# Four linked edits at the start and inside the last layer of a four-layer graph network: where input blocks are scaled, where two blocks' last sums stand, and which group's products come first

## The chip, the cores and the metric

The kernel runs on one core of a Trainium2 chip. The metric is the device time of one launch in microseconds; the time before is the median of three runs. Beside these runs there is one profiled execution, from which all views are taken. Five engines work side by side: TensorE (PE, matrix products; its weight loads are shown apart as PEld), VectorE (DVE), ScalarE (ACT), GpSimd (POOL) and SyncE (SP), which here only issues DMAs.

## The reference

The input x has 128 graphs of 64 nodes with 256 features. Four layers follow one another, each as `x = layernorm(x + layer(x))`: an attention layer, a multi-head edge attention, a graph convolution with two batch norms, and a last layer:

```python
h = relu(einsum('ts,bsh->bth', adj, x @ Wg0 + bg0))
h = relu(einsum('ts,bsh->bth', adj, h @ Wg1 + bg1))
for p in range(1, 5):                       # window length
    nw = T // p
    wins = h[:, :nw * p, :].reshape(B * nw, p, H)
    last = lstm_last(Wih[p-1], Whh[p-1], bih[p-1], bhh[p-1], wins)   # p steps, zero start
    h = h.at[:, arange(nw) * p + (p - 1), :].set(last)
```

The input of the last layer is the layer norm of the third layer's output, and that output ends in a batch norm, `out * scale + shift` for each feature. All of this is float32. The edits lie in the last layer alone.

## The kernel before

**Blocks, groups and pairs.** The nodes are worked on in 16 blocks of 512 rows (8 graphs each). Two blocks make a group of 16 graphs, two groups a pair; there are four pairs, and pair k takes blocks 4k to 4k+3. A tile `H` holds the hidden state of one pair, with the two groups side by side, and an LSTM step is computed for both groups.

**A block's way into the LSTM.** The generator `gcn` (L957) prepares one block in steps, each ending in a `yield`. Its first step issues the loads: two DMAs for the residual `x2r` (L964), and for blocks from 4 on one DMA for the third layer's output (L966). Blocks 0 to 3 have that output in SBUF already (tile `A0`, shown as A; `NA` is 4). Then for each half `a` of the block, `fetch` scales the output in place by the batch norm (two ACT instructions, L972, one for each 128 features) and turns it to have the nodes on partitions: blocks 0 to 3 by PE transposes (L979), later blocks by `turned`, which goes through DRAM. `norm` adds the residual (DVE, L985), makes the layer norm (DVE L95 to L98, POOL L86 and L100) and stores the result for later (two DMAs, L990). After both halves follow: sums over neighbours (PE L953 in `neighbours`, copied out at L1010 by DVE and L1011 by ACT), the first product in two steps (PE L1017, DVE L1019, ACT L1021), the second in two steps (PE L1029, DVE L1032), and the **last sums** over neighbours (PE L953 again), which DVE (L1040) and ACT (L1041) write into `H`. So a block of 0 to 3 has nine steps: load, two halves, sums, two, two, last sums. Blocks 0 and 2 (of these four) use PSUM banks named g, of which there are two; blocks 1 and 3 use banks named l, of which there are six, shared with the LSTM.

**The LSTM.** `lstm(pair)` yields a unit number after each piece of work. Window length 1 has units 0 to 7: units 0 to 3 serve group 0, units 4 to 7 group 1, each twelve matmul records of L1066. Lengths 2, 3 and 4 follow. The first step of such a run has no hidden state yet: `plain` (L1163) computes three gates from the input alone (PE L1174), for each half `m` of the output features and each group `g` a sum of two products, one for each half `k` of the input features. At lengths 2 and 4 both groups of one `m` share a bank (`joint`), at length 3 each has its own. Later steps (L1209) use a scheme with seven products per gate. `output` writes the state of the last step back into `H` (DVE L1139), for each half and group, in the order (m0,g0), (m1,g1), (m0,g1), (m1,g0); the next window length's `plain` reads `H`. A float32 matmul is two records in the trace.

**Order.** What an engine issues is set by a scheduler, except that `given` (L852) puts the instructions of each step behind the last one issued before on the same engine. It does so for PE, DVE, ACT and POOL, not for SP. The first blocks are advanced by a hand-written list of block numbers (L1367), one step for each entry; after the whole list come the loads of the first LSTM weights (wx and wh, L891). Blocks 2 and 3 finish as side work of pair 0, at units given by `put` (L1381). Steps put at one unit run in the order of the `put` calls.

Of the kernel before, what the change touches and what calls it, by code (L numbers as in the profile page):

```python
# [11 lines left out]
AF = mybir.ActivationFunctionType  # L12
# [9 lines left out]
KD = D // P  # L22
# [6 lines left out]
QT = 512  # L29
# [12 lines left out]
def kernel(ctx: ExitStack, tc: tile.TileContext, i, out):  # L42
    nc = tc.nc
# [44 lines left out]
    def layernorm(dst, src, n, engine):  # L88

        st = small.tile([P, n, 6], F32, name="ln_st", bufs=5)  # L90
        mv = small.tile([P, n, 2], F32, name="ln_mv", bufs=5)
        both = small.tile([P, 2, n], F32, name="ln_rs", bufs=5)
        rs, ng = both[:, 0, :], both[:, 1, :]
        for r in range(n):
            nc.vector.bn_stats(st[:, r, :], src[:, r, :])  # L95
            nc.vector.bn_aggr(mv[:, r, :], st[:, r, :])
        rsqrt(rs, mv[:, :, 1], n)
        nc.vector.tensor_scalar_mul(ng, mv[:, :, 0], -1.0)  # L98
        for r in range(n):
            engine.tensor_scalar(dst[:, r, :], src[:, r, :], ng[:, r:r + 1], rs[:, r:r + 1],  # L100
                                 op0=OP.add, op1=OP.mult)
# [13 lines left out]
    with ExitStack() as two:  # L115
# [13 lines left out]
        def bank(shape, name="m", bufs=3):  # L129
            return (psm if name == "m" else ps).tile([P] + shape, F32, name=name, bufs=bufs)  # L130
# [571 lines left out]
        sc2, sh2 = (const.tile([P, M2], F32, name=n) for n in ("sc2", "sh2"))  # L702
# [11 lines left out]
        def hidden(q, m):  # L714
            return Z[q][:, m, :] if m < 2 else Aq(q)[:, (m - 2) * QT:(m - 1) * QT]
# [16 lines left out]
        def put(q, m, p_):  # L732
            nc.scalar.activation(hidden(q, m), p_, AF.Identity, bias=b1[:, m:m + 1])
# [29 lines left out]
        bias = wd.tile([P, SKIP, 8], F32, name="bias")  # L763
# [167 lines left out]
    def turned(src):  # L931


        t = work.tile([P, 4, 4, 32], F32, name="st", bufs=ST)
        nc.vector.transpose(t, src.rearrange("p n (j t) -> p j n t", t=32))
        o = work.tile([P, 4, 4, 32], F32, name="st", bufs=ST)
        way = dram.tile([P, 4, P], F32, name="way", bufs=4)
        nc.sync.dma_start(way, t.rearrange("p j n f -> p j (n f)"))
        for j in range(4):
            nc.sync.dma_start(o[j * 32:(j + 1) * 32].rearrange("t i n f -> t i (n f)"),  # L940
                              way[:, j, :].rearrange("(i t) x -> t i x", t=32))
        return o.rearrange("p i (c m) f -> p c m i f", m=KD)
# [14 lines left out]
    def gcn(g, half, bank, name):  # L957

        q = g * 2 + half
        here = A0[:, q % NA, :]  # L960
        x2r = []
        for a in range(2):
            x2r.append(work.tile([P, 2, D], F32, name="x2r", bufs=4))
            nc.sync.dma_start(x2r[a].rearrange("p c d -> p (c d)"), x2_dram[q][:, a * 2 * D:(a + 1) * 2 * D])  # L964
        if q >= NA:
            nc.sync.dma_start(here, z_dram[q])  # L966
        yield

        def fetch(a):
            z = here[:, a * QT:(a + 1) * QT].rearrange("p (c m t) -> p c m t", c=2, m=KD)  # L970
            for m in range(KD):
                nc.scalar.activation(z[:, :, m, :], z[:, :, m, :], AF.Identity,  # L972
                                     bias=sh2[:, m:m + 1], scale=sc2[:, m:m + 1])
            if q >= NA:
                return turned(z.rearrange("p c m t -> p (c m) t"))
            xt = bank([2, D])
            for m in range(KD):
                for c in range(2):
                    nc.tensor.transpose(xt[:, c, m * P:(m + 1) * P], z[:, c, m, :], ident)  # L979
            return xt  # L980

        def norm(a, xt):
            x = x2r[a]
            xv = x.rearrange("p c (m i f) -> p c m i f", m=KD, f=32) if q >= NA else x
            nc.vector.tensor_add(xv, xt, xv)  # L985
            x3 = here[:, a * QT:(a + 1) * QT].rearrange("p (c d) -> p c d", c=2)
            layernorm(x3, x, 2, nc.gpsimd)
            for c in range(2):
                b0 = q * GQ + a * 4 + c * 2
                nc.sync.dma_start(x3_dram[b0:b0 + 2].rearrange("s t d -> (s t) d"), x3[:, c, :])  # L990

        if q >= NA:
            came = []
            for a in range(2):
                came.append(fetch(a))
                yield
            for a in range(2):
                norm(a, came[a])
                yield
        else:  # L1000
            for a in range(2):
                norm(a, fetch(a))
                yield

        x3 = here.rearrange("p (c d) -> p c d", c=PQ)
        p_ = neighbours(bank, lambda c, f: x3[:, c, f:f + 64])
        own = work if name == "hT" else late
        hT = own.tile([P, KD, QT], F32, name=name, bufs=2)
        dst = hT.rearrange("p k (c s n) -> p s (k c) n", c=PQ, s=2)
        nc.vector.tensor_copy(dst[:, 0], p_[0].rearrange("p k c n -> p (k c) n"))  # L1010
        nc.scalar.activation(dst[:, 1], p_[1].rearrange("p k c n -> p (k c) n"), AF.Copy)  # L1011
        yield
        hN = own.tile([P, KD, QT], F32, name=name, bufs=2)
        for m in range(KD):
            p_ = bank([PQ, P])
            for k in range(KD):
                nc.tensor.matmul(p_.rearrange("p c t -> p (c t)"), wg[0][:, k, m * P:(m + 1) * P], hT[:, k, :],  # L1017
                                 start=k == 0, stop=k == KD - 1)
            nc.vector.tensor_add(hN[:, m, :].rearrange("p (c t) -> p c t", c=PQ), p_,  # L1019
                                 rb[:, m:m + 1, :].to_broadcast([P, PQ, P]))  # L1020
            nc.scalar.activation(hN[:, m, :], hN[:, m, :], AF.Relu)  # L1021
            yield
        ys = []
        for a in range(2):
            p_ = bank([2, D])
            for c in range(2):
                t = (2 * a + c) * P
                for k in range(KD):
                    nc.tensor.matmul(p_[:, c, :], hN[:, k, t:t + P], wg[1][:, k, :],  # L1029
                                     start=k == 0, stop=k == KD - 1)  # L1030
            y = work.tile([P, 2, D], F32, name="st", bufs=ST)
            nc.vector.tensor_add(y, p_, bg1[:, None, :].to_broadcast([P, 2, D]))  # L1032
            ys.append(y)
            yield
        p_ = neighbours(bank, lambda c, f: ys[c // 2][:, c % 2, f:f + 64])

        if g // 2 not in Hs:
            Hs[g // 2] = input_tile()
        dst = Hs[g // 2][:, g % 2].rearrange("p k t (h c s) -> p h s k c t", h=2, s=2)[:, half]
        nc.vector.tensor_scalar_max(dst[:, 0], p_[0], 0.0)  # L1040
        nc.scalar.activation(dst[:, 1], p_[1], AF.Relu)  # L1041
        yield
# [4 lines left out]
    def lstm(pair):  # L1047
# [36 lines left out]
        for p in range(2, SKIP + 1):  # L1084
# [78 lines left out]
            def plain(n, r, tiles):  # L1163

                t = tiles[n] = rows()
                at, _ = gate_of(n)
                for m in (1, 0):
                    f, b = bias_of(n, m)
                    joint = 2 * nw * GB <= QT
                    banks = lbank([2, nw, GB]) if joint else None  # L1170
                    for g in range(2):
                        one = banks[:, g] if joint else lbank([nw, GB])
                        for k in range(KD):
                            nc.tensor.matmul(one, w.raw[0][:, k, at, m, :], inp(r, 0, k)[:, g],  # L1174
                                             start=k == 0, stop=k == KD - 1)
                        if not joint:
                            nc.scalar.activation(t[m][:, g], one, f, bias=b)
                    if joint:
                        nc.scalar.activation(t[m], banks, f, bias=b)
                for m in (1, 0):  # L1180
                    finish(n, r, 0, tiles, m)
                    tanh(n, tiles, m)
# [180 lines left out]


    parts = [gcn(n // 2, n % 2, gbank if n % 2 == 0 else lbank, "hT" if n % 2 == 0 else "xs") for n in range(4)]
    first = [prepare(weights_of[0, p]) for p in (2, 3)]
    for n in [0, 1, 0, 0, 1, 1, 0, 1, 0, 1, 2, 0, 1, 2, 0, 1, 3, 2, 0, 1, 0, 1, 3, 2, 3]:  # L1367
        given(next, parts[n])
    for part in first:
        next(part)  # L1370
# [7 lines left out]
            kind, u = key if isinstance(key, tuple) else ("at", key)  # L1378
            side.setdefault((pair, kind, u), []).append(part)

    put(0, parts[2], 0, 0, 1, 1, 2)  # L1381
    put(0, parts[3], 0, 1, 1, 2, 2, 3)
    put(0, first[0], 3, 4)
    put(0, first[1], 9, 11)

# [6 lines left out]
    for k in range(NP):  # L1392
# [5 lines left out]
        for n in range(2):  # L1398
            g = k * 2 + n
# [61 lines left out]
```

## Time and profile before

| | us |
|---|---|
| median of three runs | 2076.69 (2075.84 to 2077.88) |
| profiled execution | 2073.7 |
| its span | 2071.6 |
| PE busy | 1969.8 (95%) |
| DVE busy | 1162.1 (56%) |
| ACT busy | 956.1 (46%) |
| POOL busy | 718.6 (35%) |

The span runs from the first to the last instruction of the program; the profiled execution's time holds 2.1 us more around it. A line number is that of the kernel before. "Busy" counts the time in which an engine has an instruction at work; a matmul's end is modelled, so PE's rows overlap a little. The last layer begins at about 774 us and takes the rest of the span. In a timeline each row has its start, its length, engine, line, operation, the tiles written and read, and how many instructions of one kind were merged; a bracket gives the idle time of that engine before it and the instruction that ended it.

### The profile page before, as it was taken

The page shows a single profiled execution, that of the slowest core. Times are in us where ns is not written, and L with a number is a line of the kernel's source. Part 1 is how long each engine was busy: PE and PEld are TensorE (multiplying, and loading weights), DVE is VectorE, ACT ScalarE, POOL GpSimd, SP SyncE. Part 2 cuts the span into 40 slices and gives each one's busy share as a digit, 9 for nine tenths or more (in the row PEclk, how much of TensorE's full clock was granted, in tenths as well). Part 3 has the DMA queues.
Part 4 walks back from the last instruction along what each step waited for, and adds up shares of the span by engine and source line. Part 5 has one row for each costly group of instructions (what it writes and reads, how often), then busy time and mean ns, then how long its engine had stood idle before and what let it go on. Part 6 is the DMA issues. An engine that isn't in the chain of part 4 may idle for free.

```text
span 2071.6 us, 31358 instructions
## 1 busy us (share of the span) xinstructions
PE 1969.8 (95%) x11619; PEld 1381.3 (67%) x11619; DVE 1162.1 (56%) x2643; ACT 956.1 (46%) x1835; POOL 718.6 (35%) x890
## 2 busy tenths in 40 slices
PE   5999999998999998999999999999999999999997
PEld 4666767675454445587678587687587687586675
DVE  7456665554544445574466674466674466443556
ACT  2766666665337403544343644343644343543333
POOL 1123343343210004173545253345253345133254
PEclk9999999999999999999999999999999999999998
DMA  5354343332201127351232532032522032301012
GB/s 144 69 68 67 73 78 53 55 54 44 44 34 17 41 89 246 116 190 51 86 133 68 180 117 91 11 131 68 183 86 79 1 120 69 128 1 77 1 62 71
DMA packets 235961, 170.68 MB, mean 82 GB/s; under 512 B 150560, under 2 KB 213536, under 8 KB 232480
## 3 DMA queue, kind: packets, MB, share of 16 engines
q1 hardware_dynamic: 233952, 166.72, 29.0%
q8 instruction: 91, 1.49, 0.3%
q0 software_dynamic: 1024, 1.05, 0.2%
q10 hardware_dynamic: 832, 0.92, 0.1%
q14 instruction: 62, 0.51, 0.1%
HBM read 107.82 MB, written 60.82 MB: 81 GB/s over the span
## 4 chain that ended last, share of the span: by engine, by line
PE 75%; DVE 13%; ACT 4%; POOL 3%; issue 3%; DMA 1%; SPq 0%; DVEq 0%; POOLq 0%; ACTq 0%
PE l L1209 27%; PE l L1174 9%; PE l L1066 8%; PE pz L789 5%; PE pz L727 5%; PE e L331 3%; PE m L303 2%; PE g L1029 2%; PE m L306 2%; PE m L238 2%; PE z L340 2%; PE g L1017 1%; DVE ln_st L95 1%; PE g L953 1%; PE m L421 1%
## 5 line engine op out<-in xcount | busy, mean ns | idle before, releaser
L1209 PE MATMUL l<-xs,wx 128*128 128x256 f32 (+1 forms) x896 | 277.1, 400 | 5.2 <-DVE gate L1228 4.3
L1209 PE MATMUL l<-hs,wh 128*128 128x256 f32 (+1 forms) x896 | 275.3, 399 | 3.1 <-DVE hs L1103 3.1
L1224 ACT ACTIVATE kept<-l 128x256 f32<-128x256 f32 (+1 forms) x224 | 88.5, 402 | 340.0 <-PE l L1209 338.7
L86 POOL TENSOR_TENSOR ln_rs<-ln_rs,mhalf 128x2 f32<-128x2 f32 (+2 forms) x98 | 83.3, 850 | 462.4 <-DVE ln_rs L98 450.3
L1209 PE MATMUL l<-H,wx 128*128 128x256 f32 (+1 forms) x672 | 210.5, 402 | 3.4 <-DVE gate L1237 3.4
L1209 PE MATMUL l<-hid,wh 128*128 128x256 f32 (+1 forms) x672 | 208.9, 399 | 0.0
L1209 PEld LDWEIGHTS l<-xs,wx 128*128 128x128 f32 x896 | 169.0, 190 | 49.3 <-POOL st L100 5.3
L1209 PEld LDWEIGHTS l<-hs,wh 128*128 128x128 f32 x896 | 169.8, 190 | 45.1 <-DVE hs L1103 5.7
L1174 PE MATMUL l<-H,wx 128*128 128x256 f32 (+1 forms) x768 | 188.0, 403 | 6.1 <-DVE H L1139 6.1
L1242 ACT ACTIVATE gate<-gate,bias 128x512 f32<-128x512 f32 (+1 forms) x280 | 170.1, 656 | 35.3 <-DVE gate L1233 31.1
L1174 PEld LDWEIGHTS l<-H,wx 128*128 128x128 f32 x768 | 147.0, 193 | 46.1 <-DVE H L1139 10.4
L1066 PE MATMUL l<-H,wih 128*128 128x512 f32 x384 | 166.3, 593 | 1.7 <-DVE H L1040 1.7
L342 ACT ACTIVATE u<-z 128x1024 f32<-128x1024 f32 x128 | 130.3, 1025 | 64.3 <-PE z L340 63.5
L1209 PEld LDWEIGHTS l<-H,wx 128*128 128x128 f32 x672 | 126.2, 190 | 38.2 <-DVE gate L1237 7.4
L1209 PEld LDWEIGHTS l<-hid,wh 128*128 128x128 f32 x672 | 127.6, 191 | 31.7 <-issue 2.6
L1066 PEld LDWEIGHTS l<-H,wih 128*128 128x128 f32 x384 | 72.9, 190 | 90.4 <-issue 82.6
L1232 POOL TENSOR_TENSOR gate<-gate,kept 128x256 f32<-128x256 f32 (+1 forms) x84 | 64.9, 773 | 159.4 <-DVE kept L1230 159.4
L314 DVE TENSOR_TENSOR qs<-m,qs 64x256 fp32r<-64x256 f32 x128 | 54.0, 422 | 109.5 <-ACT qs L313 107.3
L727 PE MATMUL pz<-A,w 128*128 128x512 f32 x256 | 113.2, 596 | 0.0
L340 PE MATMUL z<-gath_r,qs 128*128 128x512 f32 x256 | 100.5, 480 | 0.6 <-ACT u L342 0.4
L1161 ACT ACTIVATE gate<-cell 128x512 f32<-128x512 f32 (+1 forms) x88 | 58.6, 666 | 81.3 <-DVE cell L1153 59.0
L1107 POOL TENSOR_TENSOR hs<-hid 128x256 f32<-128x256 f32 (+1 forms) x28 | 25.6, 915 | 200.1 <-DVE hid L1136 116.4
(277 smaller groups left out, 3632.7 us busy)
## 6 DMA issues: line engine op xcount, KB each, us to landing
wx<-sums SPq DMA_DIRECT2D x9, 2048.0 KB
wh<-sums SPq DMA_DIRECT2D x9, 1792.0 KB
way<-st SPq DMA_DIRECT2D x54, 256.0 KB
st<-way SPq DMA_DIRECT2D x216, 64.0 KB
xin<-in_x SPq DMA_DIRECT2D x16, 512.0 KB
ld<-table SPq DMA_DIRECT2D x16, 512.0 KB
x_dram<-y SPq DMA_DIRECT2D x16, 512.0 KB
x2r<-x_dram SPq DMA_DIRECT2D x32, 256.0 KB
```

The costliest lines, as they stand in the source:

```text
L86: nc.gpsimd.tensor_tensor(dst, dst, mhalf[:, :n], OP.pow)
L331: nc.tensor.matmul(pes[S][n * CG:(n + 1) * CG, :], apad[:, k, CG - HEADS - r0:2 * CG - HEADS - r0], u[:, k, :], start=r0 == 0 and k == 0, ...
L340: nc.tensor.matmul(z[:, k, :], L1[q]["qs"][c][:, s, k * P:(k + 1) * P], gath_r, start=True, stop=True)
L342: nc.scalar.activation(u, z, AF.Relu)
L727: nc.tensor.matmul(p_, w1[:, k, m * P:(m + 1) * P], Aq(q)[:, k * QT:(k + 1) * QT], start=k == 0, stop=k == KD - 1)
L789: nc.tensor.matmul(p_, w2[:, k, m * P:(m + 1) * P], hidden(q, k), start=k == 0, stop=k == M1 - 1)
L1066: nc.tensor.matmul(b, wih1[:, k, mw * P:(mw + 1) * P], Hw[:, k], start=k == 0, stop=k == KD - 1)
L1174: nc.tensor.matmul(one, w.raw[0][:, k, at, m, :], inp(r, 0, k)[:, g], start=k == 0, stop=k == KD - 1)
L1209: nc.tensor.matmul(self.banks[j], lhs, rhs, start=src == 0, stop=src == 1)
L1224: nc.scalar.activation(self.keep(j), b, AF.Copy)
L1232: e.tensor_tensor(t[0][:, 1], t[0][:, 1], k[5], OP.add)
L1242: given(lambda: nc.scalar.activation(dst, dst, f, bias=b))
```

## The change

For blocks 0 to 3 the scaling (L972) moves from `fetch` into the generator's first step, so that all four scaling instructions of a block are issued when its loads are. Later blocks keep it in `fetch`. The hand-written list advances block 0 by three steps before it begins block 1. Block 2's last sums stay at unit 2 but go behind block 3's two steps there, and block 3's last sums come from unit 3 to the end of unit 2. In `plain`, group 1's products come before group 0's.

```diff
-        if q >= NA:
-            nc.sync.dma_start(here, z_dram[q])
-        yield
-
-        def fetch(a):
-            z = here[:, a * QT:(a + 1) * QT].rearrange("p (c m t) -> p c m t", c=2, m=KD)
+        zs = [here[:, a * QT:(a + 1) * QT].rearrange("p (c m t) -> p c m t", c=2, m=KD) for a in range(2)]
+
+        def scale(a):
+            z = zs[a]
             for m in range(KD):
                 nc.scalar.activation(z[:, :, m, :], z[:, :, m, :], AF.Identity,
                                      bias=sh2[:, m:m + 1], scale=sc2[:, m:m + 1])
+
+        if q >= NA:
+            nc.sync.dma_start(here, z_dram[q])
+        else:
+            for a in range(2):
+                scale(a)
+        yield
+
+        def fetch(a):
+            z = zs[a]
             if q >= NA:
+                scale(a)
                 return turned(z.rearrange("p c m t -> p (c m) t"))
...
-                    for g in range(2):
+                    for g in (1, 0):
                         one = banks[:, g] if joint else lbank([nw, GB])
                         for k in range(KD):
                             nc.tensor.matmul(one, w.raw[0][:, k, at, m, :], inp(r, 0, k)[:, g],
...
-    for n in [0, 1, 0, 0, 1, 1, 0, 1, 0, 1, 2, 0, 1, 2, 0, 1, 3, 2, 0, 1, 0, 1, 3, 2, 3]:
+    for n in [0, 0, 0, 1, 1, 1, 0, 1, 0, 1, 2, 0, 1, 2, 0, 1, 3, 2, 0, 1, 0, 1, 3, 2, 3]:
         given(next, parts[n])
...
-    put(0, parts[2], 0, 0, 1, 1, 2)
-    put(0, parts[3], 0, 1, 1, 2, 2, 3)
+    put(0, parts[2], 0, 0, 1, 1)
+    put(0, parts[3], 0, 1, 1, 2, 2)
+    put(0, parts[2], 2)
+    put(0, parts[3], 2)
     put(0, first[0], 3, 4)
```

## The prediction

> **What bounds the kernel now.** I read the page first: the shares and the chain of work that ended last.
>
> ```profile
> PE 1969.8 (95%) x11619; PEld 1381.3 (67%) x11619; DVE 1162.1 (56%) x2643; ACT 956.1 (46%) x1835; POOL 718.6 (35%) x890
> ...
> PE 75%; DVE 13%; ACT 4%; POOL 3%; issue 3%; DMA 1%; SPq 0%; DVEq 0%; POOLq 0%; ACTq 0%
> ```
>
> TensorE (PE) is the bound. The edit takes no matmul away, so it can only close or open gaps on PE. I therefore looked for PE's gaps at the places it touches. First, PE in order of time at the start of the last layer (start, us, instruction; in brackets the idle time before it and what ended it):
>
> ```profile
> 797.97 0.93 PE L979 MATMUL g<-ident,A 128*128 128x128 f32 x4 [1.93 <-ACT A L972]
> ...
> 807.16 1.11 PE L953 MATMUL l<-bdT,st 64*64 64x64 f32 x64
> 809.88 0.93 PE L979 MATMUL l<-ident,A 128*128 128x128 f32 x4 [1.61 <-ACT A L972]
> 810.74 1.16 PE L953 MATMUL g<-bdT,A 64*64 64x64 f32 x64
> 813.19 0.93 PE L979 MATMUL l<-ident,A 128*128 128x128 f32 x4 [1.29 <-ACT A L972]
> ```
>
> Three groups of transposes (block 2's first half, then block 3's two halves) wait for L972, the scaling, and nothing else runs on PE meanwhile. The chain runs through these waits, so they are real time. ScalarE (ACT) in the same stretch:
>
> ```profile
> 793.37 0.63 ACT L1021 ACTIVATE xs<-xs 128x512 f32<-128x512 f32 x1 [1.09 <-DVE xs L1019]
> 795.08 0.63 ACT L1021 ACTIVATE hT<-hT 128x512 f32<-128x512 f32 x1 [1.09 <-DVE hT L1019]
> 796.80 0.63 ACT L1021 ACTIVATE xs<-xs 128x512 f32<-128x512 f32 x1 [1.08 <-DVE xs L1019]
> 797.33 2.06 ACT L972 ACTIVATE A<-A,sh,sc 128x256 f32<-128x256 f32 x4
> ```
>
> ACT idles a microsecond before each L1021 and the scaling runs only after the last: it is late through its place in the order, since its inputs were complete at 774.9. Next, PE around unit 3 of the first pair:
>
> ```profile
> 845.76 5.31 PE L1066 MATMUL l<-H,wih 128*128 128x512 f32 x12
> 851.00 1.16 PE L953 MATMUL l<-bdT,st 64*64 64x64 f32 x64
> 853.89 2.38 PE L1066 MATMUL l<-H,wih 128*128 128x512 f32 x5 [1.73 <-DVE H L1040]
> ```
>
> Block 3's last sums (L953) stand right before unit 4, which reads what VectorE (DVE) makes of them (L1040). Last, a start of the four-long LSTM steps, DVE and then PE:
>
> ```profile
> 1043.25 0.50 DVE L1139 TENSOR_TENSOR H<-gate 128x336 f32<-128x336 f32 x1
> ...
> 1044.27 1.33 DVE L1139 TENSOR_TENSOR H<-gate 128x336 f32<-128x336 f32 x3
> ```
>
> ```profile
> 1044.34 1.03 PE L1174 MATMUL l<-H,wx 128*128 128x256 f32 x4
> 1045.65 1.13 PE L1174 MATMUL l<-H,wx 128*128 128x256 f32 x4 [0.29 <-DVE H L1139]
> ```
>
> **What the Trainium skill says.** "PSUM — Partial Sum Buffer", Engine vs sequencer instructions: matmuls start and complete in program order, ScalarE's and VectorE's queues are strict FIFO. The trace agrees: the gaps above are whole-engine gaps. "ScalarE: Activation LUTs", What ACT_TABLE_LOAD costs: 280 ns + 0.833 ns per element, 493 ns at 256; the trace has 2.06/4 = 0.51 us each. "TensorE: Matmul & The Clock Gate", Part 1: after an idle window of about 3.4 us the array runs at half rate until a busy one. In the last pair, waits of 2.53 and 2.73 us are each followed by weight loads of 0.33 instead of 0.19 us, at 1882.2 to 1885.5 and 1964.3 to 1967.3: half rate, some 1.7 us lost each, though both waits are under the stated window.
>
> **Part 1: scaling at the load.** The sixteen scalings of blocks 0 to 3 stay sixteen. For blocks 0 and 1 the new list (0,0,0,1,1,1) leaves the order on ACT, PE, DVE and POOL as it was. For block 2 four scalings move from 797.33 into the idle time after the L1021 at 793.37: about 793.9 to 796.0. The next L1021 then starts at 795.95 rather than 795.08 and ends at 796.6. PE's L1029 reads that; but PE does the transposes first (796.05 to 796.5), then an L1029 matmul on the other half (0.43 us), so it asks at 796.9: covered by 0.3 us. Block 3's four go behind the L1021 of 796.80, where ACT idles until 807.4. Removed from PE: 1.93 + 1.61 + 1.29 = 4.83 us. Each group also has a gap inside, while the second scaling ends: 0.93 us against 0.60 for the group at 802.19 that waits for nothing, 0.33 each, 1.0 in all. **5.8 us.** What is late next: block 2's sums at 810.74 need two g banks emptied by L1040 and L1041 (until 808.5); PE's own 2.3 us of earlier gain moves those too, and block 3's transposes lie between. Unit 0 needs block 1's L1041, which ends at 809.49, shifted to about 807.2, while PE arrives at about 808. Slack 0.7 us. If these covers fail I lose up to 2 us; I see no further gain.
>
> Moved as well are two DMAs: block 1's two loads of x2r, 256 KB each, now come in program order after block 0's four stores (L990), which wait for POOL. SyncE (SP), which issues them:
>
> ```profile
> 773.36 2.22 SPq L964 DMA_DIRECT2D x2r<-x_dram  x4
> 775.99 0.38 SPq L891 DMA_DIRECT2D wx<-in_WihT  x1
> 780.71 2.99 SPq L990 DMA_DIRECT2D x_dram<-A  x4
> ```
>
> The wx load is traced after the whole list, yet it is issued before the stores: SP is filled by readiness, not by program order. The x2r tiles have four buffers, so block 1's loads are ready at once. I take **0**; the other end is the first rival.
>
> **Part 2: last sums.** The same 64 matmuls of L953 (1.1 us) go ahead of unit 3; L1040 then (1.07 us) runs under unit 3's 5.2 us of PE, and unit 4 no longer waits: **1.7 us**. Block 3's sums now follow block 3's L1029 closely and need an L1032 (0.69 us plus some 0.2 to start); block 2's sums, put between, take 1.09. Behind the moved evictions on ACT stand unit 3's gates, due 1.7 us into unit 3; two evictions of 1.08 are done by then or 0.5 us later, and a unit has 5 us. Bounds: 1.0 to 2.0.
>
> **Part 3: second group first.** The four L1139 products come in the code's order: (m0,g0), (m1,g1), (m0,g1), (m1,g0). Today's first L1174 matmul needs only the first, and so does the same product for the other bank; these are the four records (two a matmul) at 1044.34. Then PE waits for the fourth. With g1 first, and each bank filled in program order as this suggests, the first matmul needs the third product. It ends at 1045.19 (the fourth at 1045.60), so PE waits from 1044.34 to 1045.24 and then runs eight matmuls of 0.43 us: done at 1048.7, against 1045.65 + 6 x 0.43 = 1048.2. That is 0.45 us lost in each of pairs 0 to 2. In the last pair the first product ends at 1963.85 and the third at 1964.69: 0.84 lost. **Cost 2.2 us.** The two-long steps wait for nothing here. The three-long ones have a bank for each group, and PE already takes what is ready (its second matmul waits for the third product): 0. Bounds: a gain of 0.9 (the three waits of 0.29 go, if banks needn't be filled in order) to a loss of 3.7 (0.5 more at three of the three-long starts). Whether a half-rate stretch begins can add or take 1.7.
>
> **Sum.** -5.8 - 1.7 + 2.2 = -5.3 us on a span of 2071.6: 2066.3. The profiled execution took 2073.7, which is 3.0 under the median of 2076.69; the difference is taken over whole: **2071.4 us**. A measurement here tells about 0.2%, 4.2 us, from no change: faster means under 2072.5.
>
> **Rivals.**
> 1. *The loads queue behind the stores.* If SP keeps program order, block 1's x2r is issued after block 0's fourth store, at 783.8. A first load took 3.90 us to land (chain at 773.36), so the add that ran at 781.2 runs at 787.7: 6.5 us on the chain, since DVE's later work for block 0 stands behind it. An idle PE then adds a half-rate stretch, 1.7. -5.3 + 8.2 = +2.9: **2079.6, slower.** It decides once the loads are issued later than about 777. The skill's "DMA: Bandwidth & Descriptors", Anatomy of one DMA, says that a wait is served on the issuing sequencer, which speaks for blocking; the early wx load speaks against. 7%.
> 2. *Part 3 gains.* If the scheduler may start either group in a bank, PE uses the products as they come: -5.8 - 1.7 - 0.9 = -8.4: **2068.3.** Against: today PE waits for the fourth product though the third was there. 20%.
> 3. *Part 3 costs more or part 1 gives less,* by 3.7 instead of 2.2, or by a bank that isn't empty: about -3.6: **2073.1.** 25%.
>
> The forecast case has 48%. Range 2066.8 to 2075.6, which leaves out the first rival and the tails. Faster by over 0.2%: 0.70 (0.40 + 0.20 + 0.10); within: 0.23; slower: 0.07.
>
> **What would show it.** Right: no PE wait for L972 in the first 40 us of the layer; unit 0 starts some 5.8 us after the same distance from the last bn_stats; unit 4 has no wait for L1040; the four-long starts show a wait of about 0.9 us before their first L1174. Wrong: x2r loads after L990 on SP; new waits of L953 or L1066 on DVE; starts of L1174 with no wait at all.

## The result, and the profile after

| | before | after |
|---|---|---|
| median of 20 runs each, us | 2074.26 (2068.25 to 2079.13) | 2071.05 (2069.2 to 2073.79) |
| span of the profiled execution, us | 2071.6 | 2069.8 |

The ratio is 0.9984, with an interval of 0.9976 to 0.9991: a gain of 3.3 us (1.9 to 5.0). The forecast was 2071.4, a gain of 5.3. The direction is right; the gain is smaller. That 2071.05 lies so near 2071.4 is luck: the kernel before took 2074.26 here, 2.4 us under the 2076.69 that the forecast started from.

The code grew by nine lines, so most lines of the last layer stand nine further on: L1174 is now L1183, L1139 is L1148, L1066 is L1075, L1040 is L1049, L979 is L988, L990 is L999, L1017, L1021 and L1029 are L1026, L1030 and L1038. The scaling, L972, is L970.

The page's busy times have hardly moved, as they should where no work is taken away:

```profile
PE 1970.3 (95%) x11619; PEld 1379.4 (67%) x11619; DVE 1161.1 (56%) x2643; ACT 955.8 (46%) x1835; POOL 720.2 (35%) x890
```

What moved is PE's idle time. This is the timeline of PE after, at the start of the last layer:

```profile
795.78 0.60 PE L988 MATMUL g<-ident,A 128*128 128x128 f32 x4
...
805.68 0.65 PE L988 MATMUL l<-ident,A 128*128 128x128 f32 x4
806.27 1.16 PE L953 MATMUL g<-bdT,A 64*64 64x64 f32 x64
807.36 0.66 PE L988 MATMUL l<-ident,A 128*128 128x128 f32 x4
807.85 5.32 PE L1075 MATMUL l<-H,wih 128*128 128x512 f32 x12
...
834.91 3.62 PE L1038 MATMUL l<-wg,xs 128*128 128x256 f32 x16
838.46 1.16 PE L953 MATMUL g<-bdT,st 64*64 64x64 f32 x64
839.44 1.11 PE L953 MATMUL l<-bdT,st 64*64 64x64 f32 x64
840.49 20.01 PE L1075 MATMUL l<-H,wih 128*128 128x512 f32 x46
```

No row has a bracket: the three waits of transposes (L988) for the scaling are gone, and each of these groups takes 0.60 to 0.66 us instead of 0.93, so the gap inside it is gone too. The two last sums stand side by side at 838.46 and 839.44, and from 840.49 on 46 records of L1075 run as one row: unit 4 follows unit 3 with nothing between. Next, ACT after, in the same stretch:

```profile
793.27 0.63 ACT L1030 ACTIVATE xs<-xs 128x512 f32<-128x512 f32 x1 [1.09 <-DVE xs L1028]
793.81 2.06 ACT L970 ACTIVATE A<-A,sh,sc 128x256 f32<-128x256 f32 x4
795.77 0.61 ACT L1030 ACTIVATE hT<-hT 128x512 f32<-128x512 f32 x1
796.71 0.63 ACT L1030 ACTIVATE xs<-xs 128x512 f32<-128x512 f32 x1 [0.32 <-DVE xs L1028]
797.24 2.06 ACT L970 ACTIVATE A<-A,sh,sc 128x256 f32<-128x256 f32 x4
```

Block 2's four scalings fill ACT's idle time from 793.81, block 3's come from 797.24, long before PE asks for them. Then the waits of PE from 770 us to the end, after (engine and line that wait, what they wait for, us in total, times, longest):

```profile
PE l L1183 <- DVE H L1148: 10.1, 8, 3.6
```

and the same row before:

```profile
PE l L1174 <- DVE H L1139: 6.1, 5, 2.7
```

The rows for L972 (4.8 us together) and L1066 on L1040 (1.7 us) are gone. The starts of the longer steps wait at eight places instead of five, and 4.0 us longer. In the timeline of PE and then of DVE, a three-long start after:

```profile
950.12 3.09 PE L1183 MATMUL l<-H,wx 128*128 128x336 f32 x10 [0.36 <-DVE H L1148]
```

```profile
948.39 0.41 DVE L1148 TENSOR_TENSOR H<-gate 128x256 f32<-128x256 f32 x1
...
949.32 1.08 DVE L1148 TENSOR_TENSOR H<-gate 128x256 f32<-128x256 f32 x3
```

The third product is the second of the row of three; it ends at about 950.06 (products start 0.33 us apart and take 0.41), and PE's first matmul starts at 950.12. Before, the first matmul at this place waited for nothing. A four-long start after, in the same two views:

```profile
1037.57 4.80 PE L1183 MATMUL l<-H,wx 128*128 128x256 f32 x21 [0.73 <-DVE H L1148]
```

```profile
1035.59 0.49 DVE L1148 TENSOR_TENSOR H<-gate 128x336 f32<-128x336 f32 x1
...
1036.60 1.33 DVE L1148 TENSOR_TENSOR H<-gate 128x336 f32<-128x336 f32 x3
```

Here too the first matmul comes when the third product has ended, after a wait of 0.73 us where there was one of 0.29 after four records.

**Where the time went, place by place.** I took PE's instructions that are the same in both traces and subtracted their start times, after less before:

| place | us | what it adds |
|---|---|---|
| first matmul of the last layer | -0.1 | |
| unit 0 of pair 0 | -6.1 | part 1: -6.0 |
| unit 4 of pair 0 | -8.15 | part 2: -2.05 |
| ahead of the three-long start of pair 0 | -8.23 | |
| behind it / behind the four-long start | -7.66 / -7.22 | +0.57, +0.44 |
| pair 1, likewise | -6.67 / -6.24 | +0.55, +0.43 |
| pair 2, likewise | -5.68 / -5.23 | +0.56, +0.45 |
| pair 3, likewise | -3.50 / -1.31 | +1.7, +2.2 |
| end | -1.8 | -0.5 |

So in this pair of traces parts 1 and 2 bring 8.1 us, and 6.4 of them are lost again at the starts that part 3 touches. The prediction had 7.5 and 2.2.

### The profile page after: what moved, and what is told of

Same layout as the page of the kernel before. It is cut to its first block, busy times and chain, and to the rows that moved or that the text cites. A ratio compares the mean times of both kernels' runs of the same rounds, so it can differ in the third digit from the quotient of the medians.

```text
span 2069.8 us, 31352 instructions
## 1 busy us (share of the span) xinstructions
PE 1970.3 (95%) x11619; PEld 1379.4 (67%) x11619; DVE 1161.1 (56%) x2643; ACT 955.8 (46%) x1835; POOL 720.2 (35%) x890
## 4 chain that ended last, share of the span: by engine, by line
PE 75%; DVE 14%; ACT 4%; POOL 3%; issue 3%; DMA 1%; SPq 0%; DVEq 0%; POOLq 0%; ACTq 0%
PE l L1218 26%; PE l L1183 9%; PE l L1075 8%; PE pz L789 5%; PE pz L727 5%; PE e L331 3%; PE m L303 3%; PE g L1038 2%; PE m L238 2%; PE m L306 2%; PE z L340 2%; PE m L421 1%; DVE cell L1162 1%; PE g L953 1%; DVE ln_st L95 1%
## 5 line engine op out<-in xcount | busy, mean ns | idle before, releaser
L1183 PE MATMUL l<-H,wx 128*128 128x256 f32 (+1 forms) x768 | 190.0, 407 | 10.1 <-DVE H L1148 10.1
L1183 PEld LDWEIGHTS l<-H,wx 128*128 128x128 f32 x768 | 148.5, 195 | 51.7 <-DVE H L1148 16.0
L1075 PE MATMUL l<-H,wih 128*128 128x512 f32 x384 | 166.1, 593 | 0.0
L1075 PEld LDWEIGHTS l<-H,wih 128*128 128x128 f32 x384 | 72.7, 190 | 89.3 <-issue 83.0
```

The costliest lines, as they stand in the source:

```text
L1075: nc.tensor.matmul(b, wih1[:, k, mw * P:(mw + 1) * P], Hw[:, k], start=k == 0, stop=k == KD - 1)
```

## The experiments

Theory: the second group's products come late from DVE, PE begins a start with the product that the code names first even when another is ready, and so part 3 costs a wait at every three-long and four-long start (W in the expectations). Its rivals are that parts 1 and 2 lose their gain later on by themselves, and that the clock decides: the wait at a start of the last pair is followed by matmuls at half rate, and it is the length of that stretch that differs. The first four kernels below ran on one chip, the next four on a second and the last four on a third, each four beside runs of the kernel before, whose medians there were 2075.78, 2074.7 and 2077.93. In the profiles the layers ahead of the last one, which no edit touches, differ by up to 3.9 us; so places are compared within the last layer.

| label | what | median, us | ratio to before |
|---|---|---|---|
| e1_parts12 | parts 1 and 2 | 2065.11 | 0.995 (0.9936 to 0.9963) |
| e2_part3 | part 3 alone | 2080.52 | 1.0024 (1.0015 to 1.0033) |
| e3_part1 | part 1 alone | 2070.03 | 0.9969 (0.9957 to 0.9981) |
| e4_part2 | part 2 alone | 2073.78 | 0.9992 (0.9984 to 0.9999) |
| e6_only3long | 1, 2, and 3 at three-long | 2069.38 | 0.9973 (0.9963 to 0.9984) |
| e7_only4long | 1, 2, and 3 at four-long | 2067.83 | 0.9968 (0.9956 to 0.998) |
| e8_warm | 1, 2, matmuls in the waits | 2063.96 | 0.9951 (0.9938 to 0.9964) |
| e9_after_warm | after, matmuls in the waits | 2069.44 | 0.9978 (0.9969 to 0.9987) |
| e10_g1_ready | after, other order on DVE | 2069.71 | 0.9953 (0.9939 to 0.9966) |
| e11_loads_late | 1, 2, loads behind stores | 2076.28 | 0.9994 (0.9988 to 1.0001) |
| e12_after_again | after | 2074.61 | 0.9982 (0.9975 to 0.9989) |
| e13_parts12_again | parts 1 and 2 | 2066.23 | 0.994 (0.9926 to 0.9954) |

### Part 3 undone, and part 3 alone

The kernel after, with the old order of the groups in `plain`:

```diff
-                    for g in (1, 0):
+                    for g in range(2):
```

> The changed kernel with group 0's products first again, as before the change (parts 1 and 2 alone). Theory W, waits: comparing the two traces, parts 1 and 2 bring unit 4 of the first pair 8.1 us forward, and part 3 gives back 6.3 us later: 0.43 at each three-long start and 0.57 at each four-long start of pairs 0 to 2 (3.0 in all), and 3.3 in the last pair, where the longer wait is followed by a longer half-rate stretch. So the time is 8.1 us under before, a ratio of about 0.996, and 5 to 6 us under the changed kernel; the starts of the longer steps wait as before the change (0.29 at the four-long ones). Rival C, clock: the 3.3 us lost in the last pair are the phase of the clock and not part 3; then they stay here, and the time is about 4.8 us under before.

Measured: a gain of 10.4 us (7.7 to 13.3). Against the trace before, unit 4 starts 7.4 us earlier, and this lead is the same at every mark up to the last pair: nothing is lost in pairs 0 to 2. At the three-long start of the last pair it grows to 9.1, because that start has no half-rate stretch here. PE's row of waits at these starts is again that of before:

```profile
PE l L1183 <- DVE H L1148: 6.1, 5, 2.7
```

So the gain of parts 1 and 2 isn't lost by itself; part 3 takes it.

The kernel before, with only that line changed the other way:

```diff
-                    for g in range(2):
+                    for g in (1, 0):
```

> The kernel before with group 1's products first (part 3 alone). Theory W: 4 to 6 us slower than before, a ratio of 1.002 to 1.003: 3.0 us in pairs 0 to 2 by new waits of 0.37 and 0.73 at the three- and four-long starts, 1 to 3 us in the last pair with its half-rate stretches. Rival C: 3.0 us and no more. The forecast on record had 2.2 us, with nothing at the three-long starts.

Measured: a loss of 5.0 us (3.1 to 6.9). By the same marks each of pairs 0 to 2 loses 0.57 at the three-long start and 0.45 at the four-long one, and the last pair 0.57 and 0.58, 4.3 in all. The row of waits, from 770 us to the end:

```profile
PE l L1174 <- DVE H L1139: 10.1, 8, 3.6
```

It is the row of after, word for word but for the line numbers. The half-rate stretches in the last pair are no longer than before, so the 4.3 is waiting: PE works 3.4 and 2.9 us at half rate there, against 3.4 and 3.4 before. At the last four-long start the wait is 0.84 us longer (3.57 against 2.73) and the shorter half-rate work gives 0.25 of it back, hence 0.58.

### Part 1 alone, part 2 alone

After without parts 2 and 3 (the second line is undone as in e1_parts12):

```diff
-    put(0, parts[2], 0, 0, 1, 1)
-    put(0, parts[3], 0, 1, 1, 2, 2)
-    put(0, parts[2], 2)
-    put(0, parts[3], 2)
+    put(0, parts[2], 0, 0, 1, 1, 2)
+    put(0, parts[3], 0, 1, 1, 2, 2, 3)
...
-                    for g in (1, 0):
+                    for g in range(2):
```

> The kernel before with the scaling at the load and the new list (part 1 alone). Theory W: unit 0 of the first pair starts 6.1 us earlier, the wait of 1.73 us before unit 4 stays, and the time is 6 us under before (ratio about 0.997). Rival: the earlier start is met by a longer wait before unit 4, since VectorE is late there; then 4 us or less.

Measured: a gain of 6.4 us (3.9 to 8.9), and unit 0 is 5.7 us earlier against the layer's first matmul. The wait ahead of unit 4 is untouched, as the timeline of PE shows:

```profile
850.79 13.54 PE L1075 MATMUL l<-H,wih 128*128 128x512 f32 x31 [1.73 <-DVE H L1049]
```

The 1.73 in the bracket is the figure of before: part 1 moves this place and doesn't close it.

The kernel before with part 2 alone:

```diff
-    put(0, parts[2], 0, 0, 1, 1, 2)
-    put(0, parts[3], 0, 1, 1, 2, 2, 3)
+    put(0, parts[2], 0, 0, 1, 1)
+    put(0, parts[3], 0, 1, 1, 2, 2)
+    put(0, parts[2], 2)
+    put(0, parts[3], 2)
```

> The kernel before with the last sums of blocks 2 and 3 moved (part 2 alone). Theory W: the wait of 1.73 us before unit 4 is gone and nothing else moves: unit 4 starts 1.7 to 2.0 us earlier and the time is that much less, ratio about 0.999, at the edge of what can be told. Rival: the moved evictions hold back unit 3's gates and the gain is under 1 us.

Measured: a gain of 1.7 us (0.2 to 3.3); unit 4 is 2.05 us earlier against unit 0. PE's timeline:

```profile
848.67 1.16 PE L953 MATMUL g<-bdT,st 64*64 64x64 f32 x64
849.65 1.11 PE L953 MATMUL l<-bdT,st 64*64 64x64 f32 x64
850.69 13.57 PE L1066 MATMUL l<-H,wih 128*128 128x512 f32 x31
```

Both sums, then units 3 and 4 in one row, no bracket. The two parts don't depend on each other: in the profiles with part 1 unit 4 comes 2.05 us earlier still where part 2 is in, and at the same distance from unit 0 where it is not.

### Part 3 at one kind of start

Parts 1 and 2, with the new order at three-long starts only:

```diff
-                    for g in (1, 0):
+                    for g in ((1, 0) if p == 3 else (0, 1)):
```

> Parts 1 and 2, with group 1's products first at the three-long starts only. Theory W (each start pays for waiting on the third product instead of the first): 0.43 us at each of three pairs and 0.56 in the last, 1.9 us over the kernel with parts 1 and 2 alone, which was 10.4 under before; so some 8.5 under before, ratio about 0.996, and a wait of 0.37 us before each three-long start's first product, none new at the four-long ones. The forecast on record had nothing here: then it equals parts 1 and 2 alone, ratio 0.995.

Measured: against e1_parts12 each three-long start of pairs 0 to 2 costs 0.56 us and the four-long ones nothing. The waits of PE from 940 to 1730 us, which holds the six starts of these pairs, first here and then in e1_parts12:

```profile
PE l L1183 <- DVE H L1148: 2.0, 6, 0.4
```

```profile
PE l L1183 <- DVE H L1148: 0.9, 3, 0.3
```

Three new waits of 0.36 or so appear. The bracket is smaller than the loss because a row's modelled end runs some 0.2 us past the next one's start, so a short gap doesn't show whole; the difference of starts is the loss.

The same at four-long starts only:

```diff
-                    for g in (1, 0):
+                    for g in ((1, 0) if p == 4 else (0, 1)):
```

> Parts 1 and 2, with group 1's products first at the four-long starts only. Theory W: 0.57 us in each of three pairs and 0.73 in the last, 2.4 us over the kernel with parts 1 and 2 alone; ratio to before about 0.996, and a wait of 0.73 us at the four-long starts in place of 0.29. The forecast had 2.2 here. If neither this nor the three-long kernel shows a loss, part 3 costs through the clock alone.

Measured: 0.44 to 0.45 us at each four-long start, nothing at the three-long ones. The waits in the same stretch:

```profile
PE l L1183 <- DVE H L1148: 2.2, 3, 0.7
```

Still three waits, now of 0.73 instead of 0.29: 0.44 each. These two runs put the price on each kind of start separately. By medians they are 4.3 and 2.7 us above e1_parts12, which ran on another chip; the marks are the surer measure.

### The order of DVE's products

If the place in DVE's order is the cost, then giving DVE the order that PE wants should remove it. In the kernel after, the last step of a run makes its products in the order (m1,g1), (m0,g1), (m0,g0), (m1,g0):

```diff
-                        given(output, r, s, 0, o.tiles["o"], o.tiles["g"], (0,))
+                        if not last:
+                            given(output, r, s, 0, o.tiles["o"], o.tiles["g"], (0,))
...
                         given(output, r, s, 0, o.tiles["o"], o.tiles["g"], (1,))
+                        if last:
+                            given(output, r, s, 0, o.tiles["o"], o.tiles["g"], (0,))
```

> The changed kernel with the last step's products of VectorE in another order: (m1,g1), (m0,g1), (m0,g0), (m1,g0) instead of (m0,g0), (m1,g1), (m0,g1), (m1,g0), so that group 1 is complete at the second product and not at the third. Theory W (the cost of part 3 is the place of the first needed product in VectorE's order): at the starts of pairs 0 to 2 the waits of 0.37 and 0.73 shrink by the 0.33 and 0.42 us between two products, to about 0 and 0.3, and in the last pair by as much; the time is 2 to 3 us under the changed kernel. Rival (TensorE waits for the group as a whole, or for the fourth product): nothing changes.

Measured: 2069.71 us against 2074.61 of the kernel after on the same chip (e12_after_again below), 4.9 less by the medians; the spans of the two profiles differ by 1.9 (2069.9 and 2071.8), and from unit 0 on e10_g1_ready takes 3.1 us less. PE's row of waits from 770 us on:

```profile
PE l L1183 <- DVE H L1148: 7.0, 5, 3.2
```

and a four-long start of it, in PE's timeline:

```profile
1040.56 4.65 PE L1183 MATMUL l<-H,wx 128*128 128x256 f32 x20 [0.32 <-DVE H L1148]
```

The waits at the three-long starts of pairs 0 to 2 are gone, those at the four-long ones are 0.32 instead of 0.73, and 3.1 us of waiting is removed in all. Group 1 first is not bad in itself: it is bad while DVE makes group 1's products third and fourth. What is left in the last pair, 2.94 and 3.15 us, is less than after's 3.20 and 3.57 and more than before's 2.53 and 2.73, by 0.41 and 0.42: PE's first matmul needs the second product here and needed the first before, and the two start about 0.4 us apart. Whether PE waits for that one product or for both of group 1 the run can't tell, as both are there at the second.

### Half rate in the last pair

Parts 1 and 2 (the order of the groups undone as in e1_parts12), with three unused matmuls of 512 columns put into each of the two waits of the last pair, so that PE isn't idle so long:

```diff
+    def warm(n):
+        while True:
+            p_ = gbank([QT])
+            for _ in range(n):
+                nc.tensor.matmul(p_, ident, A0[:, 0, :QT], start=True, stop=True)
+            yield
...
+    put(NP - 1, warm(3), wait(22), wait(33))
```

> Parts 1 and 2, with three matmuls of 128 columns by 512 put into TensorE's wait ahead of the three- and of the four-long start of the last pair (2.6 us of work into waits of 2.5 and 2.7 us; their result is not used). Theory C2 (an idle TensorE is what starts the half-rate stretches there): no weight load of 0.33 us is left at the two starts, and the time falls by the 1.7 us of each stretch that a run has, 1 to 3 us under parts 1 and 2 alone. Rival: the stretches come whatever TensorE does, or the added matmuls end after the wait and hold the start up; then it is equal or up to 1 us slower.

Measured: 2063.96 us against 2065.11 for e1_parts12 on another chip (ratios 0.9951 and 0.995): no difference that can be told. The mechanism is there: neither start has a half-rate weight load any more. The gain isn't. Across the two starts of the last pair PE gains 1.1 us on e1_parts12, and then it waits for DVE. The waits from 1955 to 2045 us, here and then in e1_parts12:

```profile
PE l L1218 <- DVE gate L1237: 2.5, 2, 1.3
PE l L1218 <- DVE gate L1235: 1.2, 3, 0.5
```

```profile
PE l L1183 <- DVE H L1148: 2.7, 1, 2.7
PE l L1218 <- DVE gate L1237: 1.6, 2, 1.2
PE l L1218 <- DVE gate L1235: 1.0, 2, 0.5
```

The wait for H goes, and 1.1 us of new waiting for DVE's gates takes its place. In this stretch DVE is next to set the pace.

The same edit on the kernel after:

> The changed kernel with the same three matmuls in each of the last pair's two waits, which are 3.2 and 3.6 us long here. Theory W with C2: the half-rate stretches of 5.2 and 5.7 us in its trace are gone, and the time is 2 to 5 us under the changed kernel; what is left over parts 1 and 2 with the same matmuls is the pure waiting of part 3, 4.3 us. Theory W without the clock: nothing is gained, and the changed kernel stays 3.3 us under before.

Measured: 2069.44, ratio 0.9978 against 0.9984 for after itself; the intervals overlap, so the expected 2 to 5 us didn't come. Half rate is gone at both starts, and the waits at the starts fell from 10.1 to 5.0 us in all, but another half-rate stretch stands at 2002.5 to 2005.9 and waits for DVE follow as in e8_warm. How much of part 3's cost in the last pair the clock holds can't be read from this run.

### The first rival, forced

The rival that ends slower (block 1's x2r loads behind block 0's stores) didn't happen. In SyncE's timeline after, the loads are issued where they were, ahead of L999:

```profile
773.26 2.24 SPq L964 DMA_DIRECT2D x2r<-x_dram  x4
...
780.66 3.08 SPq L999 DMA_DIRECT2D x_dram<-A  x4
```

To price it, e11_loads_late is parts 1 and 2 (the order of the groups undone again) with block 1's loads ordered behind block 0's last store:

```diff
+    stores = []
...
-            nc.sync.dma_start(x2r[a].rearrange("p c d -> p (c d)"), x2_dram[q][:, a * 2 * D:(a + 1) * 2 * D])
+            with tc.issue_after(stores[-1]) if q == 1 else ExitStack():
+                nc.sync.dma_start(x2r[a].rearrange("p c d -> p (c d)"), x2_dram[q][:, a * 2 * D:(a + 1) * 2 * D])
...
+                stores.append(nc.cur_bb.bb.instructions[-1])
```

> Parts 1 and 2, with block 1's two x2r loads held behind block 0's last store on SyncE, which is the first rival of the forecast made real. The rival's price was 6.5 us on the chain and 1.7 for a half-rate stretch, so 8.2 over parts 1 and 2 alone. If the load lands faster on a queue that is quieter by then (2 us instead of 3.9), it is 4.5 to 5.

Measured: 2076.28 us, 10.05 above e13_parts12_again on the same chip, and unit 0 is 9.5 to 9.8 us later. SyncE's timeline, the chain of waits, and PE's timeline:

```profile
785.02 1.99 SPq L1002 DMA_DIRECT2D x_dram<-A  x2
787.05 2.33 SPq L967 DMA_DIRECT2D x2r<-x_dram  x4
```

```profile
787.05 5.62 DMA x2r<-x_dram
```

```profile
796.16 1.24 PE L953 MATMUL l<-bdT,A 64*64 64x64 f32 x32 [9.87 <-POOL A L100]
...
799.33 3.78 PE L1030 MATMUL g<-hT,wg 128*128 128x512 f32 x4
```

The load (merged with others in SyncE's row) is issued at 787.05 and takes 5.62 us to land instead of 3.90, so that the add which needs it comes 9.2 us later than in the kernel before, counted from the first load. PE waits 9.87 us for the normalised block, and the first product behind it (L1030 in this kernel, L1026 in the kernel after) runs at half rate for longer: four records in 3.78 us, where after has 2.94 for the same four and 1.88 for the next four. Had it come so, parts 1 and 2 would have been undone.

### After and parts 1 and 2, once more on one chip

Neither is edited.

> The changed kernel once more, beside parts 1 and 2 alone on one chip. Theory W: 0.2% under before, and 5 to 7 us over parts 1 and 2 alone.

> Parts 1 and 2 alone once more, on the chip of the run before: 8 to 10 us under the kernel before, ratio 0.995 to 0.996. If it comes out within 3 us of the changed kernel, the cost of part 3 found so far was a difference between chips.

Measured: 2074.61 and 2066.23. Part 3 costs 8.4 us here by the medians, 6.9 by the spans of the profiles (2071.8 and 2064.9). By the marks, 3.0 of this lie in pairs 0 to 2, 3.6 at the three-long start of the last pair and 0.7 at its four-long start. That 3.6 is 0.57 of waiting, and for the rest the clock, which the profile records as it was granted. In every trace here it is either full or half, and apart from the ends of the record the times between its changes are whole multiples of 3.41 us: it is set anew step by step. The rows below show such steps around that start: from and to, length, PE's busy time (records), the granted share of the clock, then DMA. First e12_after_again, next e13_parts12_again, last e2_part3:

```profile
1874.80:1878.22 3.42, 0.94 (x5) 1.00 0.55 139
1878.22:1881.63 3.41, 2.69 (x5) 0.50 1.05 447
1881.63:1885.04 3.41, 3.41 (x7) 0.50 0.96 410
1885.04:1888.46 3.42, 3.42 (x13) 1.00 0.40 164
```

```profile
1871.51:1874.93 3.42, 1.64 (x8) 1.00 0.42 86
1874.93:1878.34 3.41, 2.67 (x9) 1.00 0.95 399
```

```profile
1885.66:1889.07 3.41, 1.38 (x5) 1.00 0.87 360
1889.07:1892.49 3.42, 3.42 (x8) 0.50 1.00 426
1892.49:1895.90 3.41, 3.41 (x13) 1.00 0.73 306
```

In the first, PE works 6.1 us at half rate and so loses half of that; in the second none, though PE waited 2.53 us; in the third 3.4 us, though it waited as long as in the first (3.2 us). All 24 starts of the last pair in the profiles without added matmuls fit one reading: where PE was busy for 1.4 us or less of a step, the next step came at half rate (19 starts), and where for 1.6 us or more, it did not (5). The half rate lasted one step where PE filled at least 2.9 us of it (13) and two where it filled 2.8 or less (6). Elsewhere in the layer steps with 1.4 to 1.7 us of work went either way. This was read off the traces afterwards; no run shifted a start along the steps to test it.

Parts 1 and 2 without part 3 are faster than both kernels: on this chip 0.994 of before against 0.9982. Only e8_warm, which is the same with added matmuls, has a lower median, and the two can't be told apart.

## Why the prediction was right or wrong

**Part 1: right.** 5.8 was forecast, 6.0 and 5.7 were read from the traces of after and of part 1 alone, and 6.4 from the runs of part 1 alone. Of the ten profiles with this part and without held loads, eight have 5.6 to 6.0; in e7_only4long and e10_g1_ready it is 3.9 and 3.7, where the layer's first product (L1026) runs at half rate for longer, four records in 3.78 us against 2.94; that is a part of the difference, and the rest was not followed. The placement came as worked out: block 2's scalings at 793.81 (forecast 793.9), the next L1030 at 795.77 (795.95), and the covers held, since neither L1038 nor unit 0 waits. (The 493 ns quoted from "ScalarE: Activation LUTs" is that section's figure for one operand read through a pointer, and the scaling has two; nothing hung on it, as the trace's 2.06 us for four was used.) That the rearranged list by itself does nothing, as the prediction takes it, was not run separately.

**Part 2: right.** 1.7 was forecast, 1.7 measured by runs and 2.05 by trace, just over the bound of 2.0. The forecast took the bracket of 1.73 as the whole gap; as at the three-long starts, a row's modelled end hides a little of it.

**Part 3: the sign right, the size wrong.** Three terms of it:

- *Four-long starts of pairs 0 to 2, 0.45 each:* measured 0.44. The first matmul waits for the third product, as worked out. The wait is 0.73 where about 0.9 was said, as rows overlap.
- *Three-long starts, "a bank for each group, and PE already takes what is ready": 0.* **This step failed.** It was argued from one trace in which a second matmul waited for the third product; it was read as "takes what is ready". In the changed kernel the first matmul waits for the third product, though the first product was done more than a microsecond before. The order is thus fixed ahead of the run, with the product first that the code names first. It isn't the code's order throughout: before, in the last pair, the second matmul starts at 1881.51, right behind the third product (until 1881.46), while the code's own second one needs the fourth (until 1881.79). A start loses the one matmul that used to run ahead of the third product, two records that start 0.28 us apart: 0.57 us at all four starts, 2.3 in all. The bound that I gave for it, 0.5 at three starts, was too low as well.
- *Last pair, four-long, 0.84:* right. The wait went from 2.73 to 3.57 us. That e2_part3 loses only 0.58 there comes from its shorter half-rate work.

The waiting comes to 4 x 0.57 + 3 x 0.44 + 0.84 = 4.4 us, against 2.2 forecast and 3.7 as the upper bound; e2_part3 has 4.3, with 0.25 given back by the clock.

**The clock: taken as even, it came one-sided.** The prediction let half rate "add or take 1.7". In the last pair PE works 12.0 us at half rate in the trace of after (5.8 and 6.2 at its two starts) and 6.8 in that of before, which is (12.0 - 6.8) / 2 = 2.6 us lost. With 4.4 of waiting that makes 7.0, and 0.5 is won back behind the last start; the marks have 6.4 in all. The same sum, with half-rate work of 9.0 and 3.2 us, gives 4.3 for the last pair of e12_after_again over e13_parts12_again, where the marks have 4.3; for e2_part3 over before it gives 1.2, and the marks have 1.1. So the clock's part runs from -0.2 to 2.9 us, by where the two waits fall on the steps of 3.41 us. A longer wait empties a step more often: all ten starts with waits of 2.9 to 3.6 us had half rate behind them, of fourteen with 2.5 to 2.7 us nine. The Trainium skill, "TensorE: Matmul & The Clock Gate", Part 1, puts the fall to half rate after an idle window of about 3.4 us. The steps of 3.41 us agree with it; here a step in which PE worked for up to 1.4 us counted as idle, so waits shorter than the window were enough. What the clock is worth by an experiment stays open: e8_warm and e9_after_warm removed the half rate, and waits for DVE hid the gain.

**The sum.** In the trace, -8.15 + 6.35 gives the 1.8 between the spans. The runs have -3.3 (-1.9 to -5.0). By the trace parts 1 and 2 were undersized by 0.6, part 3 by 2.8 (its runs alone, 5.0) to 4.2 (the trace, 6.4). By the medians e1_parts12 and e13_parts12_again gain more, 10.4 and 11.7; in both profiles the last three-long start has no half rate, which is 1.7 of it. What came is the third rival and not the forecast case: a gain of 3.3, where that rival has about 3.6 (its own terms, 5.8 + 1.7 - 3.7, make 3.8). It named part 3 as the doubtful term; of its two reasons the first was right, and "a bank that isn't empty" was seen nowhere. The gain is 0.16%, so it also fell under the 0.2% to which the prediction gave 0.70. The range held because it reached to this rival.

**The rivals.** That part 3 gains is ruled out by the starts in the trace: they wait longer, not less. The loads behind the stores didn't occur; forced, they cost about 10 us rather than 8.2. The add came 9.2 us later instead of 6.5, as the load was issued about 0.9 us later than assumed and took 5.62 us to land and not 3.90; little came on top of that, as unit 0 is 9.5 to 9.8 us later in all.

## What to carry to other kernels

Where one engine makes several parts and another uses them, let the order of use be the order of making: swapping only one side cost a wait at every start here, and swapping the other side as well (e10_g1_ready) took back 3.1 of the 4.0 us of added waiting. Work that was late only through its place in an engine's queue was worth the whole gap once it stood in an idle stretch, and this could be read and added up ahead of the edit from brackets in the timeline. "It takes what is ready" must be shown for each shape before a term is set to 0: at both kinds of start PE waited for the product that the code names first while another was ready.

## What the runs showed of the hardware that I had not expected

- The granted clock changes on steps of 3.41 us, and half rate followed waits of only 2.5 to 2.7 us at nine of fourteen starts: what went with it is how much PE worked within one step (1.4 us or less before half rate, 1.6 or more without), not the length of the wait alone. Float32 weight loads take 0.33 to 0.34 us at half rate, against 0.19 at full rate.
- Three unused matmuls in such a wait were enough to keep the full rate at that start (e8_warm, e9_after_warm), and gained nothing that can be told, since DVE was next.
- In one trace (e11_loads_late) a 256 KB load took 3.89 us to land when issued at 775.67 and another of that size 5.62 when issued at 787.05, with other loads and stores issued around it.
